# A quarter of layer 2's softmax tokens moved onto the partitions in three of sixteen samples

## The chip, the core and the metric

The kernel runs on one core of a Trainium2 chip. The metric is the device time of one launch in microseconds (us). The engines have short names here: TensorE (PE; its weight loads are PEld), VectorE (DVE), ScalarE (ACT), GpSimd (POOL), SyncE (SP). SP issues most of the DMA transfers, ACT issues some, POOL issues the gathers.

## The reference, cut to what matters

A batch of 16 samples of 64x64 tokens with 256 channels goes through four residual layers. Layer 0 replaces each token by its nearest of 1024 codes and adds it, layer 1 is attention along image rows with a sigmoid, layer 2 is the one changed here, and layer 3 is linear attention. Each layer starts with a group norm.

```python
def _L2_conv_ref(x, w1, b1, w2, b2, w3, b3):
    n = h * w                                     # 4096 tokens
    x0 = jnp.einsum('bnc,c->bn', xf, w1) + b1[0]
    x1 = jnp.einsum('bnc,c->bn', xf, w2) + b2[0]
    x2 = jnp.einsum('bnc,c->bn', xf, w3) + b3[0]
    sim = x0[:, :, None] * x1[:, None, :]
    sm = jax.nn.softmax(sim, axis=1)
    feats = jnp.einsum('bn,bnm->bm', x2, sm)
    gate = jax.nn.sigmoid(feats).reshape(b, h, w, 1)
    return gate * x
...
x = x + _L2_conv_ref(_gn(x), ...)
```

For each token m the kernel needs two sums over all 4096 tokens n: the denominator, sum of exp(x0[n]*x1[m] - max), and the numerator, the same sum weighted by x2[n]. That is 4096 x 4096 exponentials for each sample.

## The kernel before, in words

Everything is written with the Tile framework: the program is traced once as a flat list of instructions, and an offline scheduler then fixes one order for each engine's queue. On the chip each queue is worked off in that order, and an instruction waits there for what it needs. The trace order comes from generators (one for each stage of each sample) which a heap at the end of `tile_net_kernel` interleaves by due times: about one sample's time of `stage1` (layer 0, "search"), `layer1`, `rows2` and `stage2` (layer 2's rows and exponentials, "exps"), `gate2` and `stage3` (layer 3). In the middle of the run, stages of up to four samples are in work at once. At the start only the search and the exponentials overlap. At the end, sample 15 has nothing behind it.

- `stage1`, lines 398 to 415: for each of 32 token tiles, four f32 products of 512 columns into a two-bank PSUM tile `pd` (L403), a bias row on ACT (`nn`, L398), two DVE passes (L409, L414) and a gather by POOL (L415). The two-bank tiles come from the pool `ps_w`, which has two buffers; `layer1` takes its `ph` and `po` from it as well.
- `rows2`: x0, x1, x2 of a sample as three rows. `x01` holds x0 and x1 with tokens on the partitions (token tile T in column T), and the rows go to DRAM (`rd`).
- `spread_rows` (L613 to L617): loads half the tokens (2048) of x0 and of x2, each repeated over all 128 partitions, as `x0b` and `x2b`.
- `stage2` (from L620): for each half h and each token tile T, ACT computes `ex` = exp(x0 * x1[m] - max) for the 128 tokens m of the tile on the partitions and 2048 tokens n along the free axis, summing as it goes (L645, `den`); DVE multiplies by `x2b` and sums (L648, `num`). The tile `ex` has three buffers. So one sample has 64 pairs of one ACT and one DVE instruction. I call such a pair an exponential and its product. After them come `gate` (L656 to L663), a transpose (L666) and a store to DRAM (L669), from which `gate2` reads it back (L695).
- Samples 0 to 14 compute their gate once at the end (`parts=1`). Sample 15 goes in eight parts of four token tiles, each through both halves, so that its `gate2` can start early.
- `layer1` (L482, `pfg`) and `rows2` (L593, `pr`) have products with 32 output columns, which stand beside each other in four groups of PSUM partitions.

Of the kernel before, what the change touches and what calls it, by code (L numbers as in the profile page):

```python
# [9 lines left out]
F32 = mybir.dt.float32  # L10
BF16 = mybir.dt.bfloat16
U32 = mybir.dt.uint32
AF = mybir.ActivationFunctionType
ALU = mybir.AluOpType
AX = mybir.AxisListType

P = 128
C = 256
NK = C // P
TOK = 4096  # L20
NT = TOK // P
CH = 4
NCHUNK = NT // CH
CW = CH * P
# [12 lines left out]
LAG4 = 0.04  # L37
LEN3 = {0: 0.4, 1: 0.33, 2: 0.37}
FILL = ((0.05, 0.95, 2), (1.0, 1.27, 3), (1.4, 1.58, 2))
EARLY = sum(n for _, _, n in FILL)  # L40


@with_exitstack
def kernel(
# [7 lines left out]
    nc = tc.nc  # L52
# [3 lines left out]
    const = ctx.enter_context(tc.tile_pool(name="const", bufs=1))  # L56
# [5 lines left out]
    s2p = ctx.enter_context(tc.tile_pool(name="s2p", bufs=1))  # L62
# [7 lines left out]
    def bank(name):  # L70
        return ps_m.tile([P, 512], F32, tag="pm", name=name)

    def wide(name):
        return ps_w.tile([P, 1024], F32, tag="pw", name=name)
# [40 lines left out]
    PARTS = 3  # L115
# [16 lines left out]
    def busy(t, n):  # L132

        for _ in range(n):
            nc.tensor.matmul(
                t[:, :512], lhsT=ones3, rhs=ones3.unsqueeze(1).to_broadcast([P, 4, P]), start=True, stop=True,
                skip_group_check=True,
            )

    h_row, qv_row, x_row = row_tile("h_row"), row_tile("qv_row"), row_tile("x_row")  # L140

# [425 lines left out]
    def rows2(b):  # L567
        tag = f"r2_{b}"
        scale, nmean, _ = norm2[b]
        with tc.high_priority(offset=URGENT):  # L570
            pb = bank(f"pbr_{tag}")
            busy(pb, 3)
            for k in range(NK):
                nc.scalar.activation(
                    wrow_n[:, k, :].rearrange("p (j n) -> p j n", n=32)[:, :, 0:3],
                    wrow_raw[:, k : k + 1, 0:3].to_broadcast([P, 4, 3]), AF.Copy, scale=scale[:, k : k + 1],
                )
            for k in range(NK):
                nc.tensor.matmul(
                    pb[:, 0:1], lhsT=wrow_n[:, k, :], rhs=nmean[:, k : k + 1], start=(k == 0), stop=(k == NK - 1)  # L580
                )
            brow_n = small.tile([P, 1], F32, tag="brow_n", name=f"brow_{tag}")
            nc.scalar.activation(brow_n, pb[:, 0:1], AF.Identity, bias=brow)
        x01 = small.tile([P, NT, 2], F32, tag="x01", name=f"x01_{tag}", bufs=2)
        rd = dram.tile([3, 2, 4, CW], F32, tag="rows", name=f"rows_{tag}", bufs=3)
        for h in range(2):
            pr = bank(f"pr_{tag}_{h}")
            for j in range(4):
                xt = xb.tile([P, NK, CW], F32, tag="xb", name=f"xr_{tag}_{h}_{j}")
                nc.sync.dma_start(out=xt, in_=x2_d[b][4 * h + j])  # L590
                part = slice(32 * j, 32 * j + 32)
                for k in range(NK):
                    nc.tensor.matmul(  # L593
                        pr[part, :], lhsT=wrow_n[:, k, part], rhs=xt[:, k, :], start=(k == 0), stop=(k == NK - 1)
                    )
            rows = s1p.tile([P, CW], F32, tag="t4", name=f"rows_{tag}_{h}", bufs=3)
            nc.scalar.activation(rows, pr, AF.Identity, bias=brow_n)
            for n in range(3):
                nc.scalar.dma_start(out=rd[n, h], in_=rows[n : n + 97 : 32, :])
            pt = bank(f"prt_{tag}_{h}")  # L600
            for t in range(CH):
                nc.tensor.transpose(pt[:, t * P : (t + 1) * P], rows[:, t * P : (t + 1) * P], ident)
            nc.vector.tensor_copy(
                x01[:, 16 * h : 16 * h + 16, :].rearrange("p (j t) n -> p j t n", t=CH),
                pt.rearrange("p (t j n) -> p j t n", j=4, n=32)[:, :, :, 0:2],
            )
            yield 4
        rows_d[b] = x01, rd, [spread_rows(rd, b, 0)]

    def spread_rows(rd, b, h):  # L610

        x0b = s2p.tile([P, TOK // 2], F32, tag="x0b", name=f"x0b_{b}_{h}", bufs=2)
        x2b = s2p.tile([P, TOK // 2], F32, tag="x2b", name=f"x2b_{b}_{h}", bufs=2)  # L613
        for dst, n in ((x0b, 0), (x2b, 2)):
            nc.sync.dma_start(
                out=dst, in_=rd[n : n + 1, h, :, :].rearrange("o j n -> o (j n)").to_broadcast([P, TOK // 2])
            )  # L617
        return x0b, x2b

    def stage2(b, parts=1):  # L620

# [5 lines left out]
        nc.vector.tensor_reduce(ext[:, 1:2], x01[:, :, 0], AX.X, ALU.min, negate=True)  # L627
        ab = small.tile([P, 2], F32, tag="ab", name=f"ab_{tag}", bufs=1)
        nc.gpsimd.partition_all_reduce(ab, ext, P, bass_isa.ReduceOp.max)
        nmax = small.tile([P, NT], F32, tag="nmax", name=f"nmax_{tag}", bufs=1)  # L630
        nc.vector.tensor_scalar(nmax, x01[:, :, 1], ab[:, 0:1], -1.0, ALU.mult, ALU.mult)
        nc.vector.scalar_tensor_tensor(nmax, x01[:, :, 1], ab[:, 1:2], nmax, op0=ALU.mult, op1=ALU.min)
        den = small.tile([P, 2, NT], F32, tag="den", name=f"den_{tag}", bufs=1)
        num = small.tile([P, 2, NT], F32, tag="num", name=f"num_{tag}", bufs=1)
        halves.append(spread_rows(rd, b, 1))
        gd = dram.tile([NT, P], F32, tag="gate", name=f"gd_{tag}")
        gates_d[b] = gd
        yield 2
        rest = gate2(b) if parts > 1 else None
        for part in range(parts):  # L640
            those = range(part * NT // parts, (part + 1) * NT // parts)
            for h, (x0b, x2b) in enumerate(halves):
                for T in those:
                    ex = s2p.tile([P, TOK // 2], F32, tag="ex", name=f"ex_{tag}_{h}_{T}", bufs=3)
                    nc.scalar.activation(  # L645
                        ex, x0b, AF.Exp, bias=nmax[:, T : T + 1], scale=x01[:, T, 1:2], accum_out=den[:, h, T : T + 1]
                    )
                    nc.vector.tensor_tensor_reduce(  # L648
                        out=ex, in0=ex, in1=x2b, scale=1.0, scalar=0.0, op0=ALU.mult, op1=ALU.add,
                        accum_out=num[:, h, T : T + 1],  # L650
                    )
                    yield 2.4
            n = len(those)
            cols = slice(those[0], those[0] + n)
            gate = small.tile([P, NT], F32, tag="gate", name=f"gate_{tag}_{part}", bufs=1)[:, 0:n]
            nc.vector.tensor_tensor(gate, den[:, 0, cols], den[:, 1, cols], ALU.add)  # L656
            nc.vector.reciprocal(gate, gate)
            nsum = small.tile([P, NT], F32, tag="nsum", name=f"nsum_{tag}_{part}", bufs=1)[:, 0:n]
            nc.vector.tensor_tensor(nsum, num[:, 0, cols], num[:, 1, cols], ALU.add)
            nc.vector.tensor_tensor(gate, gate, nsum, ALU.mult)  # L660
            nc.scalar.activation(gate, gate, AF.Exp, scale=-1.0)
            nc.vector.tensor_scalar(gate, gate, 1.0, None, ALU.add)
# [270 lines left out]
    b = 0  # L933
# [71 lines left out]
```

## Time and profile before

| | |
|---|---|
| median of 3 runs | 5671.16 us (5653.28 to 5692.56) |
| the profiled execution | 5674.06 us, span of its instructions 5672.1 us |
| busy PE, DVE, ACT, POOL | 91%, 89%, 81%, 32% of the span |
| mean granted TensorE clock | 0.962 of full speed |
| DMA | 1059 MB, mean 187 GB/s |
| exponentials of sample 0, first to last start | 322 to 582 us |
| exponentials of sample 14 | 4958 to 5216 us |
| exponentials of sample 15 | 5224 to 5505 us |

The profiled execution takes 2.9 us more than the median. "Busy" is the share of the span in which an engine had an instruction in work. Matmuls are pipelined, so the mean duration of one is longer than what it takes from the engine; the busy time of a group divided by its count is the better price in a stream. An f32 product is recorded as two matmul instructions, a bf16 product or a transpose as one.

### The profile page before, as it was taken

To read this page: it belongs to the slowest core of one execution; us is meant where nothing else is said; L and a number is where in the kernel's file an instruction comes from. 1 tells how busy PE (TensorE), PEld (TensorE's weight loads), DVE (VectorE), ACT (ScalarE), POOL (GpSimd) and SP (SyncE) were. 2 spreads that over 40 slices of the span, in tenths; PEclk is the share of its full clock that TensorE was granted. 3 is DMA by queue.
4 is the path that set the end of the run, shared out by engine and by line. 5 is a ranking of instruction groups with operands and counts; after the bars stand their busy time and mean duration, and the time that the engine had idled before them with its cause. 6 is when DMAs were issued, how large, how long until landed. Compare 5 with 4: busy or idle time off the path is not lost.

```text
span 5672.1 us, 76096 instructions
## 1 busy us (share of the span) xinstructions
PE 5162.0 (91%) x26927; PEld 3189.6 (56%) x26927; DVE 5049.3 (89%) x7186; ACT 4571.1 (81%) x6642; POOL 1801.5 (32%) x1076
## 2 busy tenths in 40 slices
PE   7977889989999999999999999999999999987788
PEld 3534446545656566565655656565565656564556
DVE  7589799899999999999999999999999999988882
ACT  4468589888989898888978888898888879887873
POOL 2223234323333333334333333333333333321221
PEclk9988999999999999999999999999999999998889
DMA  8553744655665757566575656657575675745543
GB/s 254 174 178 84 232 115 144 214 163 185 196 198 175 224 159 236 171 211 198 185 234 155 216 185 200 210 173 236 160 224 183 201 219 156 222 149 176 200 157 119
DMA packets 521365, 1059.26 MB, mean 187 GB/s; under 512 B 52504, under 2 KB 266392, under 8 KB 512792
## 3 DMA queue, kind: packets, MB, share of 16 engines
q1 hardware_dynamic: 406288, 885.11, 46.5%
q0 software_dynamic: 73728, 67.14, 8.3%
q10 hardware_dynamic: 40968, 102.13, 4.6%
q8 instruction: 214, 3.51, 0.3%
q14 instruction: 167, 1.37, 0.1%
HBM read 751.18 MB, written 303.04 MB: 186 GB/s over the span
## 4 chain that ended last, share of the span: by engine, by line
PE 46%; DVE 17%; ACT 16%; issue 6%; DMA 5%; POOL 4%; SPq 0%; ACTq 0%; DVEq 0%; POOLq 0%
PE pd_s L403 14%; ACT ex_s L645 7%; DVE ex_s L648 7%; PE ph_l L493 4%; PE pxo_s L908 3%; PE pqv_s L782 3%; PE po_l L533 2%; PE pk_s L765 2%; ACT nn_s L398 2%; POOL qv_s L802 2%; PE pz_s L857 2%; DVE i_s L414 2%; DVE nn_s L409 2%; PE pxo_s L902 2%; PE pvr_s L865 2%
## 5 line engine op out<-in xcount | busy, mean ns | idle before, releaser
L648 DVE CUSTOM_DVE_ANT_0 ex_s<-ex_s,x2b 128x2048 f32<-128x2048 f32 x1024 | 2360.4, 2312 | 77.6 <-ACT ex_s L645 74.6
L645 ACT ACTIVATE ex_s<-x0b,nmax_s,x_r 128x2048 f32<-128x2048 f32 x1024 | 2138.6, 2089 | 40.7 <-DVE num_s L648 30.5
L403 PE MATMUL pd_s<-e,xn_s 128*128 128x512 f32 x4096 | 1971.1, 614 | 43.9 <-DVE m L409 27.9
L415 POOL DMA_INDIRECT xc_s<-in_emb_rows,i_s x512 | 1113.7, 2175 | 1852.7 <-DVE i_s L414 1337.5
L403 PEld LDWEIGHTS pd_s<-e,xn_s 128*128 128x128 f32 x4096 | 745.8, 195 | 778.8 <-issue 669.1
L409 DVE CUSTOM_DVE_ANT_0 nn_s<-pd_s,nn_s 128x1024 f32<-128x1024 f32 x512 | 619.9, 1212 | 113.5 <-PE pd_s L403 63.0
L414 DVE FIND_INDEX8 i_s<-m,nn_s 128x8 uint32<-128x1024 f32 x512 | 622.9, 1217 | 0.0
L398 ACT ACTIVATE nn_s<-ne,nx_s 128x1024 f32<-128x1024 f32 x512 | 582.5, 1143 | 33.1 <-DVE nx_s L369 18.7
L493 PE MATMUL ph_l<-wh_l,xt_l 128*128 128x256 f32 x2048 | 519.6, 390 | 28.7 <-DVE m L409 16.9
L782 PE MATMUL pqv_s<-wqv_s,xk_s 128*128 128x256 f32 x2048 | 489.3, 381 | 0.0
L493 PEld LDWEIGHTS ph_l<-wh_l,xt_l 128*128 128x128 f32 x2048 | 379.7, 192 | 138.9 <-issue 69.0
L782 PEld LDWEIGHTS pqv_s<-wqv_s,xk_s 128*128 128x128 f32 x2048 | 389.1, 191 | 120.6 <-issue 59.7
L802 POOL TENSOR_TENSOR qv_s<-qv_s,qm_s 128x512 f32<-128x512 f32 x128 | 221.6, 1731 | 662.6 <-DVE qm_s L801 363.2
L868 POOL TENSOR_TENSOR lrs_s<-lrs_s,mhalf 128x4 f32<-128x4 f32 x128 | 178.0, 1391 | 677.2 <-ACT lrs_s L867 663.3
L756 POOL TENSOR_TENSOR qv_s<-qv_s,qd_s 128x512 f32<-128x512 f32 x128 | 214.4, 1675 | 249.0 <-DVE qd_s L755 132.0
L533 PE MATMUL po_l<-blk,h_l 128*128 128x128 f32 x2048 | 282.1, 288 | 3.0 <-DVE m L409 1.5
L533 PEld LDWEIGHTS po_l<-blk,h_l 128*128 128x128 f32 x2048 | 260.6, 200 | 41.1 <-issue 24.5
L908 PE MATMUL pxo_s<-wctx_s,qo_s 128*128 128x256 f32 x1024 | 269.2, 386 | 2.2 <-DVE qo_s L876 2.2
L765 PE MATMUL pk_s<-xk_s,wk_s 128*128 128x512 f32 x512 | 256.0, 620 | 1.0 <-DMA xk_s<-x_g 0.9
L913 ACT COPY y_s<-pxo_s 128x512 f32<-128x512 f32 x256 | 147.5, 580 | 132.4 <-PE pxo_s L912 116.0
L378 PE MATMUL pt_s<-ident,xc_s 128*128 128x128 f32 x1024 | 156.7, 282 | 105.2 <-DMA xc_s<-in_emb_rows,i_s 79.0
L351 ACT ACTIVATE sq_s<-xt_s,first 128x512 f32<-128x512 f32 x256 | 200.2, 806 | 37.2 <-DMA x0b<-rows_r 21.0
(206 smaller groups left out, 7322.0 us busy)
## 6 DMA issues: line engine op xcount, KB each, us to landing
xs_s<-in_xT SPq DMA_DIRECT2D x128, 512.0 KB
xt_s<-in_xT SPq DMA_DIRECT2D x128, 512.0 KB
xc_s<-in_x SPq DMA_DIRECT2D x128, 512.0 KB
x_s<-xt_s ACTq DMA_DIRECT2D x128, 512.0 KB
xt_l<-x_s SPq DMA_DIRECT2D x128, 512.0 KB
x_l<-xt_l SPq DMA_DIRECT2D x128, 512.0 KB
xr_r<-x_l SPq DMA_DIRECT2D x128, 512.0 KB
xg_g<-x_l SPq DMA_DIRECT2D x128, 512.0 KB
```

Of the source, the lines that this page charges most:

```text
L398: nc.scalar.activation(nn, ne2, AF.Identity, bias=nx2[ch][:, t : t + 1])
L403: nc.tensor.matmul(pd[:, cols], lhsT=xn[ch][:, k, t * P : (t + 1) * P], rhs=e2[:, k, cols], start=(k == 0), stop=(k == NK - 1),)
L409: nc.vector.tensor_tensor_reduce(out=nn, in0=pd, in1=nn, scale=1.0, scalar=-3.0e38, op0=ALU.add, op1=ALU.max, accum_out=m8[:, 0:1],)
L414: nc.vector.max_index(i8, m8, nn)
L415: nc.gpsimd.indirect_dma_start(out=xc[ch][:, t, :], out_offset=None, in_=emb_rows, in_offset=bass.IndirectOffsetOnAxis(ap=i8[:, 0:1], axis=0),
L493: nc.tensor.matmul(ph[:, t, :], lhsT=X[:, k, t * P : (t + 1) * P], rhs=wh_n[:, k, :], start=(t % 2 == 0 and k == 0), stop=False, skip_grou ...
L533: nc.tensor.matmul(po[:, m : m + P], lhsT=h[:, t, k * P : (k + 1) * P], rhs=at[:, t, :, :].rearrange("p r i -> p (r i)"), start=True, stop ...
L645: nc.scalar.activation(ex, x0b, AF.Exp, bias=nmax[:, T : T + 1], scale=x01[:, T, 1:2], accum_out=den[:, h, T : T + 1])
L648: nc.vector.tensor_tensor_reduce(out=ex, in0=ex, in1=x2b, scale=1.0, scalar=0.0, op0=ALU.mult, op1=ALU.add, accum_out=num[:, h, T : T + 1],)
L765: nc.tensor.matmul(pk, lhsT=wk_n[:, k, :], rhs=xt[:, k, :], start=(k == 0), stop=(k == NK - 1))
L782: nc.tensor.matmul(pqv[:, j, :], lhsT=xt[:, k, t * P : (t + 1) * P], rhs=wqv_n[:, k, :], start=(j == 0 and k == 0), stop=False, skip_group ...
L908: nc.tensor.matmul(px[:, j, :], lhsT=qT[:, t * P : (t + 1) * P], rhs=wctx[:, 1, :], start=False, stop=False, skip_group_check=True,)
```

## The change

In samples 0, 14 and 15 the last 1024 of the 4096 tokens n (K = 8 token tiles) leave the pairs of `stage2`. The second half's `x0b` and `x2b` are loaded with 1024 columns, and its 32 exponentials and products have 1024 columns instead of 2048. The 1024 tokens are laid on the partitions instead, in eight tiles of 128:

- `parts_of_rows`: x1, x0 of those tiles and the negated maximum are put side by side (`cat`), transposed by PE, and split into three bf16 parts on DVE (`bits`). Seven transfers write them to DRAM with runs of 128 bf16 values, and four bring the x0 parts and ones into `spread`.
- `begin`: for each chunk of 512 tokens m (eight in a sample), four transfers bring the 12 rows of parts into `uu` (two buffers), once for each group of partitions.
- `outer`: the exponent x0[n]*x1[m] - max[m] as a bf16 product with 12 rows of depth, two of 512 columns into one two-bank tile `pet` of `ps_w`; four such tiles a chunk.
- `powers`: ACT takes the exponential of such a bank pair, 1024 columns from PSUM, into a tile `et` that uses the three buffers of `ex`; two such tiles a chunk.
- `contract`: eight f32 products with 32 output columns (x2 and ones), four groups of PSUM partitions beside each other, then an ACT copy.
- `collect`: four transposes and a small DVE reduction into `sums`.

Samples 1 to 13 keep the old form; `den` and `num` become slices of `sums` for all samples, and the two additions of L656 and L659 become reductions.

```diff
+SHARE = 0
+SHARES = {0: 8, 14: 8, 15: 8}
+PROD = 12
...
-        x01 = small.tile([P, NT, 2], F32, tag="x01", name=f"x01_{tag}", bufs=2)
+        x01 = small.tile([P, NT, 3], F32, tag="x01", name=f"x01_{tag}", bufs=2)
...
+        width = TOK // 2 - (P * SHARES.get(b, SHARE) if h == 1 else 0)
...
+        def parts_of_rows():
+            nc.vector.tensor_copy(cat[:, 0:NT], x01[:, :, 1])
+            nc.vector.tensor_copy(cat[:, 2 * NT : 2 * NT + K], x01[:, NT - K :, 0])
+            nc.vector.tensor_copy(pair[:, 0:K, 0], x01[:, NT - K :, 2])
+            n = 2 * NT + K
+            pp = bank(f"pcat_{tag}")
+            nc.tensor.transpose(pp[:n, :P], cat[:, :n], ident)
+            for m in range(PARTS):
+                nc.vector.tensor_copy(bits[:n, m, :], pp[:n, :P])
+                if m + 1 < PARTS:
+                    nc.vector.tensor_tensor(pp[:n, :P], pp[:n, :P], bits[:n, m, :], ALU.subtract)
...
+        def begin(c):
+            u = s2p.tile([P, CW], BF16, tag="uu", name=f"uu_{tag}_{c}", bufs=2)
+            src = ud.rearrange("i m t p -> (i m) (t p)")[:, c * CW : (c + 1) * CW]
+            for g in range(4):
+                nc.sync.dma_start(out=u[32 * g : 32 * g + PROD, :], in_=src)
...
+        def outer(c, n):
+            pw = wide(f"pet_{tag}_{c}_{n}")
+            for r in range(2):
+                g = 2 * q + r
+                rows = slice(32 * g, 32 * g + PROD)
+                nc.tensor.matmul(
+                    pw[:, r * CW : (r + 1) * CW], lhsT=spread[rows, e, :], rhs=u[rows, :], start=True, stop=True
+                )
...
+        def powers(c, n):
+            if q == 0:
+                others[c].append(s2p.tile([P, TOK // 2], F32, tag="ex", name=f"et_{tag}_{c}_{e}", bufs=3))
+            nc.scalar.activation(others[c][-1][:, 2 * q * CW : 2 * (q + 1) * CW], banks.pop((c, n)), AF.Exp)
+
+        def contract(c):
+            pn = bank(f"pn_{tag}_{c}")
+            for e in range(K // 4):
+                for g in range(4):
+                    nc.tensor.matmul(
+                        pn[32 * g : 32 * g + 32, :], lhsT=pair[:, 4 * e + g, :],
+                        rhs=others[c][1 + e][:, g * CW : (g + 1) * CW], start=(e == 0), stop=(e == K // 4 - 1),
+                    )
+            nc.scalar.copy(others[c][-1][:, 0:CW], pn)
+
+        def collect(c):
+            pt = bank(f"pnt_{tag}_{c}")
+            for t in range(CH):
+                nc.tensor.transpose(pt[:, t * P : (t + 1) * P], row[:, t * P : (t + 1) * P], ident)
+            nc.vector.tensor_reduce(
+                sums[:, :, 2, c * CH : (c + 1) * CH].rearrange("p r t -> p t r"),
+                pt.rearrange("p (t j n) -> p t n j", j=4, n=32)[:, :, 0:2, :], AX.X, ALU.add,
+            )
...
-                    yield 2.4
+                    yield 2.4 * width / (TOK // 2)
+                    c = part + step // 8
+                    n = step % 8
+                    if K == 0:
+                        pass
+                    elif n <= K // 2:
+                        if n > 0:
+                            powers(c, n - 1)
+                            yield 1.2
+                        if n < K // 2:
+                            outer(c, n)
+                    elif n == 5:
+                        contract(c)
+                        if c + 1 < NCHUNK:
+                            begin(c + 1)
+                    elif n == 7:
+                        collect(c)
+                    step += 1
```

So one chunk spreads over eight pairs of the old loop: exponents in steps 0 to 3, their exponentials in steps 1 to 4, the sums in step 5, their collection in step 7.

## The prediction

> **What bounds the kernel now.** I read the windows view first, cut at the group norms that open layer 1, 2 or 3 of a sample, since these are points every engine passes. After the window and its length it gives each engine's busy time, the granted TensorE clock, the DMA share and GB/s.
>
> ```profile
> 322.00:493.00 171.00, 107.13 (x303) 47.95 (x301) 163.77 (x215) 130.72 (x145) 53.18 (x25) 0.83 0.42 123
> 493.00:677.00 184.00, 163.01 (x902) 93.68 (x902) 156.31 (x224) 134.76 (x194) 47.22 (x25) 0.94 0.58 176
> 2000.00:2500.00 500.00, 477.81 (x2591) 301.52 (x2590) 473.49 (x668) 438.97 (x637) 172.95 (x96) 0.99 0.61 189
> 4913.00:5190.00 277.00, 233.73 (x1343) 157.04 (x1341) 243.93 (x316) 226.25 (x335) 66.51 (x41) 0.92 0.56 184
> 5190.00:5541.00 351.00, 263.26 (x1219) 186.29 (x1218) 288.82 (x420) 265.28 (x405) 83.18 (x54) 0.86 0.50 168
> ```
>
> The engines stand as PE, PEld, DVE, ACT, POOL. In the middle (2000 to 2500) PE is busy for 96% and DVE for 95%. In the stretch where sample 0's exponentials begin (S1, to sample 1's layer 1) DVE is busy for 96%, PE for 63%. In S2 (to the norm after that layer) PE leads with 89%. In the two late ones, S4 and S5, which end at the norms that open layer 3 of samples 13 and 15, all three lie between 75% and 88%, DVE ahead. So only in S1 does one engine bound alone.
>
> Next the groups, for prices: mean ns after the busy time.
>
> ```profile
> L648 DVE CUSTOM_DVE_ANT_0 ex_s<-ex_s,x2b 128x2048 f32<-128x2048 f32 x1024 | 2360.4, 2312 | 77.6 <-ACT ex_s L645 74.6 <-issue 2.5
> L645 ACT ACTIVATE ex_s<-x0b,nmax_s,x_r 128x2048 f32<-128x2048 f32 x1024 | 2138.6, 2089 | 40.7 <-DVE num_s L648 30.5 <-DVE nmax_s L632 7.4 <-ACT xt_s L381 0.4
> L409 DVE CUSTOM_DVE_ANT_0 nn_s<-pd_s,nn_s 128x1024 f32<-128x1024 f32 x512 | 619.9, 1212 | 113.5 <-PE pd_s L403 63.0 <-ACT nn_s L398 42.7 <-PE pbr_r L579 2.7
> L398 ACT ACTIVATE nn_s<-ne,nx_s 128x1024 f32<-128x1024 f32 x512 | 582.5, 1143 | 33.1 <-DVE nx_s L369 18.7 <-DVE i_s L414 11.2 <-ACT xt_s L381 0.4
> L482 PE MATMUL pfg_l<-xt_l,wfg_l 128*32 128x256 f32 x2048 | 144.6, 389 | 6.2 <-ACT qv_s L787 3.7 <-DMA xt_l<-x_s 2.4
> L502 ACT COPY h_l<-ph_l 128x1024 f32<-128x1024 f32 x128 | 129.6, 1013 | 67.2 <-PE ph_l L498 64.9
> L498 PE MATMUL ph_l<-h_row,ones 128*128 128x512 bf16 x256 | 98.1, 383 | 0.0
> L593 PE MATMUL pr_r<-xr_r,wrow_n 128*32 128x512 f32 x512 | 91.5, 613 | 8.0 <-DMA xr_r<-x_l 7.9
> L135 PE MATMUL prow_x_s<-ones 128*128 128x512 bf16 x128 | 30.2, 379 | 0.0
> ```
>
> Last the chain that ended last, its pieces added by engine:
>
> ```text
> 325 to 500:    DVE 61%, ACT 7%,  PE 2%,  the rest issue, DMA, POOL
> 500 to 675:    DVE 14%, ACT 35%, PE 23%, DMA 20%
> 4950 to 5200:  DVE 18%, ACT 33%, PE 32%
> 5200 to 5500:  DVE 40%, ACT 14%, PE 25%
> ```
>
> I use these as weights: work that an engine gains or loses moves the end by about its share of the chain, unless it becomes the bound.
>
> **What one changed sample costs.** *DVE.* A full product is 2.31 us plus its accumulator read of 0.08, together 2.39. A half one is 1.21 (L409, 1024 columns) plus 0.08. So 32 x 1.10 = 35.2 us go. Added: `bits`, five instructions from PSUM at some 0.3 (L834, 128x128 from PSUM, has 0.289 and L809 0.340), three small copies at 0.15, eight reductions at 0.2 (L603 has 0.174): 3.6. Net -31 us. *ACT.* Full exponential 2.09 + 0.19 accumulator read = 2.28, half 1.14 (L398) + 0.19 = 1.33: 32 x 0.95 = 30.4 go. A `powers` lies between 1.01 (L502, a copy from two banks) and 1.14 (L398), I take 1.08: 34.6. Eight copies of a bank at 0.58 (L913): 4.6. Net +9. *PE.* An exponent product: 0.24 in a stream (L135, 30.2/128), 0.38 alone, below that 0.12 if the two of a bank pair, which use other rows of the array, run at once; taken 0.30: 64 x 0.30 = 19.2. A product of `contract`: L482 has 144.6/1024 = 0.14 us for one f32 product of 256 columns beside its neighbours, doubled for 512 columns 0.28; L593 gives 91.5/256 = 0.36; taken 0.28, since neighbours change group as in L482: 64 x 0.28 = 17.9. 32 transposes at 0.16 (L744, 82.7/512): 5.1. With `cat` +42.5 us, bounds 31 and 53. *SP.* 43 more issues at some 0.35 us (gate reads: 0.32) make 15 us; the two loads of 1 MB shrink to half, so bytes hardly rise.
>
> **Where it falls.** The order of both programs' queues, instruction by instruction, is the same (but for a few neighbours swapped on POOL) from the end of S2 until shortly before sample 14's exponentials. I counted the instructions between the norms and priced them as above:
>
> ```text
>                           DVE                          ACT                            PE
> S1   full products 40 -> 30: -21   full 42 -> 31, +16 powers, +3 copies: -6  +15
> S2   24 -> 2 full, 32 half: -10    22 -> 1 full, 32 half, +16, +5: +15       +27
> S4   56 -> 35 full: -53            62 -> 40 full, 12 half, +23, +5: -6       +29
> S5   83 -> 40 full, 64 half: -9    74 -> 32 full, 52 half, +41, +11: +24     +56
> ```
>
> Sample 0's pairs are put later against sample 1's search, and in S4 so much moves behind sample 13's layer 3 that S5 keeps nearly its DVE work. DVE is saturated in S1, so there -21 counts for more than its chain share of 61% (-13): I take -17. PE has 64 us free there, which hide its +15. S2: -10 x 0.14 + 15 x 0.35 + 27 x 0.23 = +10. A cross-check by throughput: PE 163 + 27 = 190 us at the 96% of the middle needs 198 us, +14. S4: -53 x 0.18 - 6 x 0.33 + 29 x 0.32 = -2. S5: -9 x 0.40 + 24 x 0.14 + 56 x 0.25 = +14, and this holds the end of sample 15, where contraction, copy, transposes and reduction (some 3.7 us) now stand ahead of the last gate. After S5 layer 3 of sample 15 (5541 to 5672) is as before. Sum -17 + 10 - 2 + 14 = +5 us, on 5674 of the profiled execution 5679, on the median 5676. With PE's bounds (31 and 53 of 42.5) the three PE terms, 29 us together, become 21 or 36, so +5 becomes -3 to +12. The whole middle costs nothing: two reductions replace two additions, 0.15 to 0.18 us each.
>
> **New waits.** The chain to the first exponents (transpose, `bits`, a store, a load) is two DMA hops; the gate's own store and read took 7.2 us from issue (597.1) to the reader's start (604.3). Until then ACT has its first two exponentials and a dozen instructions of the search in its queue, 15 us, which hide it. In SP's queue every `uu` load from the third chunk on waits for PE to finish the chunk two before; behind it stand loads of sample 2's search and, in sample 14, the second store and fifth load of layer 1 of sample 15. If these come late, ACT's norms and PE's layer 1 wait next. I take 0 and bound it by 16 chunk loads x 3 us = 48 us above and nothing below. `pet` takes one of two `ps_w` buffers from the search in S1 and S2: in S1 PE waits 10 us for `m` (L409) now; taken within S2's +10, bounded by the same 10 us again.
>
> The clock rows show 0.83 in S1 and 0.86 in S5 against 0.99 in the middle. The Trainium skill, "TensorE: Matmul & The Clock Gate", Part 1 (the HAM clock gate), says that the gate only knows half and full speed and opens after some 3.4 us of sustained work; more PE work would then make the old PE work shorter. By that rule S5's 263 busy us would shrink by up to 14%, at PE's share of the chain -9 us, and the sum would be -4.
>
> Against the change speaks "DMA: Bandwidth & Descriptors", Specifications: transfers under 512 B miss line rate, and the new stores have runs of 256 B. No row here times such a store. By its fixed cost of about 2 us a transfer, an estimate from that page, the two hops are 4 us instead of 7.2, and the sum does not move.
>
> **Rivals.** *DVE bounds all four stretches.* For it: DVE is ahead in S1, S4 and S5, and 40% of the late chain is DVE. Against it: 75 to 89% for PE, and ACT loses nothing. All of -21 - 10 - 53 - 9 = -93 on the path gives 5578; two thirds of it, 5609. *The three buffers of `ex` bind (slower).* An `et` tile holds a buffer from its first `powers` to `contract`, the second to `collect`. So in two or three of each eight steps one buffer is left, and ACT and DVE must take turns: 24 chunks x 2.5 steps x 2.3 us less a quarter for half width is 104 us if nothing else stands between, 52 if every second is filled. ACT already waited 14.5 us on the product in S1 and S2:
>
> ```profile
> ACT ex_s L645 <- DVE num_s L648: 14.5, 16, 1.6
> ```
>
> Columns: total, times, longest. Against it: the queues place other work between those exponentials. It decides from half unfilled on; with +75 us 5746. *The transfers come late.* It isn't the sums that count but the 48 us of SP above: 5719.
>
> **How the numbers follow.** A measurement of this kernel can tell about 1% (57 us) from no change. Forecast (no change to tell): 0.56. DVE rival: 0.20, faster. Buffers: 0.19, slower. Late transfers: 0.05, half on each side of the 1%. So faster 0.20, same 0.58, slower 0.22. The forecast's time is 5676; its own range, with the bounds on PE, `pd` and transfers, is 5640 to 5728. Reaching to the DVE rival's 5609 and near the buffers' 5746 leaves out some 2 in 10: 5610 to 5740.
>
> **What would show it.** Right: sample 1's layer 1 opens some 17 us earlier, its end about 7 us earlier, DVE falls below 80% in S4, PE rises above 85% in S5 with a higher clock, POOL unchanged. Wrong: waits of ACT exponentials on DVE above 60 us (buffers); waits of PE on `uu` or `spread`, or of ACT norms on `xt` (transfers); S4 and S5 together shorter by over 40 us with DVE still ahead (the DVE rival). The weights would be wrong if S5 neither grows nor shrinks although PE's work there rose by a fifth.

## The result, and the profile after

The changed kernel takes 5723.77 us (median of 7 runs, 5705.56 to 5731.39) against 5671.16 us for the kernel before on the same chip (median of 7 runs). The ratio is 1.0084, with a 95% interval of 1.006 to 1.0109: some 48 us more, 34 to 62. That is inside the forecast's range and under the 1% that it called no change to tell, but the sum had +5. The profiled execution took 5730.76 us, with a span of 5729.0.

The windows of the changed kernel, cut at the same group norms as before (S1, S2, a piece of the middle, S4, S5; columns as in the prediction). S1 opens with sample 0's first exponential, here at 319.8 us, before at 322.3:

```profile
320.00:490.00 170.00, 121.67 (x394) 50.52 (x393) 143.74 (x203) 123.08 (x144) 50.42 (x25) 0.86 0.42 121
490.00:686.00 196.00, 184.26 (x1040) 97.53 (x1041) 149.16 (x251) 149.57 (x236) 42.34 (x26) 0.97 0.54 166
2000.00:2500.00 500.00, 474.00 (x2563) 296.51 (x2562) 471.53 (x671) 434.06 (x634) 174.57 (x98) 0.99 0.60 188
4938.00:5234.00 296.00, 257.93 (x1494) 166.34 (x1493) 215.60 (x313) 221.46 (x347) 58.12 (x42) 0.92 0.51 173
5234.00:5596.00 362.00, 299.08 (x1522) 196.48 (x1520) 257.94 (x455) 285.91 (x481) 58.94 (x53) 0.90 0.49 160
```

DVE lost what it was meant to lose: 20 us in S1, 7 in S2, 28 in S4, 31 in S5 by these rows, 86 in all. No stretch got shorter by more than 2 us for it; S2 grew by 12, S4 by 19, S5 by 11. In S4 and S5 every engine but PE now has over a fifth of the stretch idle.

The groups, one form to a line, give the prices (mean ns after the busy time):

```profile
L744 DVE CUSTOM_DVE_ANT_0 ex_s<-ex_s,x2b 128x1024 f32<-128x1024 f32 x96 | 120.2, 1255 | 45.5 <-ACT ex_s L740 45.2
L740 ACT ACTIVATE ex_s<-x0b,cat_s,x_r 128x1024 f32<-128x1024 f32 x96 | 118.8, 1238 | 8.6 <-DVE sums_s L744 5.2 <-PE pn_s L710 3.2
L704 ACT ACTIVATE et_s<-pet_s 128x1024 f32<-128x1024 f32 x96 | 97.0, 1018 | 10.7 <-PE pet_s L695 10.2 <-ACT fac_s L938 0.2
L710 PE MATMUL pn_s<-et_s,pair 128*32 128x512 f32 x384 | 65.9, 630 | 1.2 <-ACT et_s L704 1.2
L695 PE MATMUL pet_s<-uu_s,spread 12*128 12x512 bf16 x192 | 41.0, 410 | 22.8 <-ACT et_s L704 19.4 <-DVE xt_l L549 2.4 <-DVE m L420 1.0
L720 PE MATMUL pnt_s<-ident,et_s 128*128 128x128 f32 x96 | 16.1, 286 | 2.8 <-ACT et_s L714 2.8
L714 ACT COPY et_s<-pn_s 128x512 f32<-128x512 f32 x24 | 13.8, 577 | 11.2 <-PE pn_s L710 10.9
```

An exponent product took 41.0/192 = 0.21 us, a product of `contract` 65.9/192 = 0.34, a transpose 0.17. Together they are 123 us of new PE work. From the waits of the whole run (total, times, longest):

```profile
DVE ex_s L744 <- ACT ex_s L740: 169.5, 142, 4.7
ACT ex_s L740 <- DVE sums_s L744: 23.9, 31, 2.4
```

Before, these two were 74.6 and 30.5. So DVE's relief came back as waits of the products on the exponentials, and the exponentials do not wait more for the products. The chain that ended last shows what stands in DVE's place. I added its pieces by engine over each whole stretch, for both kernels in the same way; in the changed kernel it doesn't reach back to S1 and S2:

```text
             before                       after
S4     PE 31%, ACT 30%, DVE 17%     PE 57%, ACT 12%, DVE 11%
S5     DVE 36%, PE 27%, ACT 15%     PE 46%, ACT 31%, DVE 13%
```

### The profile page after: what moved, and what is told of

It is laid out like the page before. It is cut to its first block, busy times and chain, and to the rows that moved or that the text cites. A ratio compares the mean times of both kernels' runs of the same rounds, so it can differ in the third digit from the quotient of the medians.

```text
span 5729.0 us, 77808 instructions
## 1 busy us (share of the span) xinstructions
PE 5253.1 (92%) x27602; PEld 3209.3 (56%) x27602; DVE 4962.7 (87%) x7234; ACT 4591.5 (80%) x6762; POOL 1764.5 (31%) x1083
## 4 chain that ended last, share of the span: by engine, by line
PE 42%; ACT 14%; DVE 10%; DMA 4%; issue 4%; POOL 3%; ACTq 0%; SPq 0%; POOLq 0%; DVEq 0%
PE pd_s L414 11%; ACT ex_s L740 6%; PE ph_l L504 4%; PE pxo_s L1021 3%; DVE ex_s L744 3%; PE pqv_s L895 3%; PE po_l L544 2%; PE pk_s L878 2%; PE pz_s L970 2%; PE pxo_s L1015 2%; PE pvr_s L978 2%; POOL qv_s L915 2%; ACT nn_s L409 2%; DVE nn_s L420 1%; DVE i_s L425 1%
## 5 line engine op out<-in xcount | busy, mean ns | idle before, releaser
L744 DVE CUSTOM_DVE_ANT_0 ex_s<-ex_s,x2b 128x2048 f32<-128x2048 f32 (+1 forms) x1024 | 2261.3, 2213 | 171.9 <-ACT ex_s L740 169.5
L740 ACT ACTIVATE ex_s<-x0b,cat_s,x_r 128x2048 f32<-128x2048 f32 (+1 forms) x1024 | 2057.0, 2009 | 47.6 <-DVE sums_s L744 23.9
L915 POOL TENSOR_TENSOR qv_s<-qv_s,qm_s 128x512 f32<-128x512 f32 x128 | 205.9, 1609 | 710.2 <-DVE qm_s L914 364.5
L869 POOL TENSOR_TENSOR qv_s<-qv_s,qd_s 128x512 f32<-128x512 f32 x128 | 196.2, 1532 | 221.9 <-DVE qd_s L868 123.2
```

What stands on the lines that cost most here:

```text
L740: nc.scalar.activation(ex, x0b, AF.Exp, bias=nmax[:, T : T + 1], scale=x01[:, T, 1:2], accum_out=sums[:, 1, h, T : T + 1],)
L744: nc.vector.tensor_tensor_reduce(out=ex, in0=ex, in1=x2b, scale=1.0, scalar=0.0, op0=ALU.mult, op1=ALU.add, accum_out=sums[:, 0, h, T : T ...
```

## The experiments

All have the changed kernel as their base unless told otherwise. The letters in the expectations stand for these theories. A: the new PE work sets the loss. D: the fixed steps of a chunk (a hop from engine to engine eight times a sample) set it, however large they are. F: transfers and SP's queue. G: ACT is the engine that holds the time after the change. H: exponent tiles take the search's PSUM buffers. B: in the first run, that what the change does in all sixteen samples costs something; in the last one, that DVE's relief is worth its share. C and E stand beside their runs.

Every kernel was compared with the kernel before, run on the same chip beside it. A ratio of 0.001 is 5.7 us. The intervals are some 0.1 to 0.25% to each side, so two experiments have to differ by some 0.3% before I call them different.

```text
                                         ratio    95% interval       us against before
the changed kernel                       1.0084   1.0060 to 1.0109   +48
no sample takes the new path             1.0013   0.9998 to 1.0027    +7
sample 0 alone                           1.0029   1.0017 to 1.0041   +16
samples 14 and 15 alone                  1.0068   1.0050 to 1.0086   +39
K = 4                                    1.0075   1.0051 to 1.0100   +43
sums as bf16 products                    1.0093   1.0071 to 1.0114   +53
exponent products twice                  1.0126   1.0112 to 1.0141   +72
preparation and transfers alone          1.0006   0.9996 to 1.0017    +3
uu three chunks ahead                    1.0090   1.0076 to 1.0105   +51
half of the powers left out              1.0074   1.0054 to 1.0093   +42
copy of the sums on DVE                  1.0080   1.0061 to 1.0099   +45
exponents in one-bank tiles              1.0128   1.0108 to 1.0149   +73
DVE's relief without the new path        0.9936   0.9915 to 0.9957   -36
```

### Which samples make the loss

```diff
-SHARES = {0: 8, 14: 8, 15: 8}
+SHARES = {}                     # first run
+SHARES = {0: 8}                 # second
+SHARES = {14: 8, 15: 8}         # third
```

> SHARES is empty: no sample takes the new path; what is left of the change is x01 with three columns, the sums tile and the two reductions per gate. Theory A (PE's added work and the places where it stands in the order make the loss): the time is that of before within 10 us (5661 to 5681), and the middle between sample 1's layer 1 and sample 14's layer 1 takes 4236 us as before, so the 17 us by which the middle grew in the profile of after are gone. Rival B (the changes that touch all sixteen samples cost something, and that is where the 17 us of the middle come from): 5680 to 5695, with the middle at 4245 to 4253.

> Only sample 0 takes the new path. Theory A: S1 -1 to -3 us, S2 +12, the rest as before: +8 to +12 us on before's time, so 5679 to 5684. If the drift of the middle is started by sample 0's new path (Theory A2): +25, 5696. Rival C (the loss is made at the end alone, and sample 0's -17 of the prediction is real and only hidden by one profile): within 5 us of before.

> Samples 14 and 15 alone take the new path. Theory A: S4 +19 and S5 +10, a little in the tail: +25 to +32 us on before, 5696 to 5703. Theory A2 (the middle's drift hangs on sample 0): the same +30 here, and the two parts together give after's +48. Rival C (DVE's relief pays at the end): within 8 us of before.

Measured: +7 us (-1 to +15), +16 (10 to 23) and +39 (28 to 49). Less the first, sample 0 costs 9 and the late pair 32; with the 7 that makes 48. The parts add up within their intervals, and the loss is made where the new path runs. Theory C falls in both its places. Theory A had 8 to 12 us for sample 0 and 25 to 32 for the pair: both measured values lie above, with intervals that still reach those figures; A2's 25 for sample 0 lies outside. The steps of the walls say the same: S2 is 198 us with sample 0 alone, and S4 is 305 with the late pair alone.

The 17 us by which the middle grew in the profile of the changed kernel are another matter. Without any new path the middle took 4247 us in its profile, against 4235 before and 4253 after, which is B's number for the middle, while the time lies at A's end. In the thirteen profiles of changed kernels it lies between 4235 and 4257, with the same PE and DVE work within 0.4%. So most of those 17 us belong to no sample's new path. A part may be a real cost of the third column of `x01` and the new reductions (the +7 above, whose interval still holds zero), the rest is what one execution differs from the next. Which part is which stays open.

### Half the tokens

```diff
-SHARES = {0: 8, 14: 8, 15: 8}
+SHARES = {0: 4, 14: 4, 15: 4}
```

> K is 4 in place of 8 in all three samples: 512 tokens on the partitions, half the exponents, powers and f32 sums, but the same transfers, bits, copies and transposes. Theory A (the price is PE work of outer and contract, which halves): half of after's loss, +20 to +28 us, 5691 to 5699. Rival D (the price is in the fixed steps of a chunk: waits of the queues at the transfers, at the copy and at the transposes): at least +40, 5710 or more. Rival E (buffers of ex): with one et tile a chunk in place of two the loss falls to under +10.

Measured: +43, within the interval of the whole change. Theory E falls, since one `et` tile a chunk in place of two gives nothing back. By its text theory D was met; but the text forgot that half the tokens also bring half of DVE's relief. That had to be known first, and the last experiment measures it.

### The transfers

```diff
 # preparation alone: full width, and of the steps only the loads
+        width = TOK // 2
...
-                    elif n <= K // 2:
-                        ...
                     elif n == 5:
-                        contract(c)
                         if c + 1 < NCHUNK:
                             begin(c + 1)
-                    elif n == 7:
-                        collect(c)
```

> The new path's preparation alone: transpose of cat, bits, the eleven transfers of the parts and the 32 loads of uu per changed sample, while all exponentials and products stay full width and exponents, powers, sums and collection are left out. Theory A: +0 to +8 us on the kernel with SHARES empty, so 5681 to 5690. Rival F (SP's queue and the waits on transfers carry the loss): +25 to +40 on it, 5706 to 5722.

```diff
 # loads three chunks ahead
-name=f"uu_{tag}_{c}", bufs=2)
+name=f"uu_{tag}_{c}", bufs=4)
...
-            begin(0)
+            for c in range(3):
+                begin(c)
...
-                        if c + 1 < NCHUNK:
-                            begin(c + 1)
+                        if c + 3 < NCHUNK:
+                            begin(c + 3)
```

> uu has four buffers and its loads are issued three chunks ahead, so that a load in SP's queue waits for PE's block four chunks before and no longer two. Theory A: within 6 us of after, 5718 to 5730. Rival F: the waits of SP on the exponent products (20 us each in samples 0 and 14 in after's trace) go, and the time falls by 15 to 40 us, to 5684 to 5709.

The first cost nothing that can be told (+3 us, -2 to +10): the transposition of `cat`, `bits`, the two hops and 43 issues a sample are hidden. In that run no load waits for an exponent product, so it says nothing of such waits. The second run does, and didn't help (+51). SP's waits on the exponent products, in its own queue, first in the changed kernel, then with the earlier loads:

```profile
SPq L683 <- PE pet_s L695: 70.4, 14, 20.1
```

```profile
SPq L683 <- PE pet_s L695: 39.0, 8, 9.5
```

They fell by 31 us and no time came of it; 39 us of them are left. Theory F's ranges are out in both runs, and with them the forecast's rival of late transfers.

### More and less PE work

```diff
 # sums as bf16 products
-    pair = const.tile([P, 8, 32], F32, name="pair")
+    pair = const.tile([P, 8, 32], BF16, name="pair")
...
-s2p.tile([P, TOK // 2], F32, tag="ex", name=f"et_{tag}_{c}_{e}", bufs=3)
+s2p.tile([P, TOK // 2], BF16, tag="ex", name=f"et_{tag}_{c}_{e}", bufs=3)
...
-            nc.scalar.copy(others[c][-1][:, 0:CW], pn)
+            row = s1p.tile([P, CW], F32, tag="t4", name=f"row_{tag}_{c}", bufs=3)
+            nc.scalar.copy(row, pn)
+            others[c].append(row)
```

> The exponentials of the tokens on the partitions are kept as bf16 and their sums are bf16 products in place of f32 ones (numbers less precise; the copy of the sums goes to a tile of its own). In after's trace the 192 f32 products took 65.9 us; 192 bf16 products over as many columns (the exponents) took 41.0, so PE should lose some 25 us or more over the three samples. Theory A (PE's added work sets the loss): time falls by 12 to 25 us against after, to 5699 to 5712. Rival D (fixed steps and queue order): within 6 us of after, 5718 to 5730.

```diff
 # exponent products twice
             for r in range(2):
...
-                nc.tensor.matmul(
+                for _ in range(2):
+                    nc.tensor.matmul(
```

> Every exponent product is issued twice into the same bank: 192 more bf16 products at 0.21 us, 41 us of PE work over the three samples and nothing else. Theory A: the time grows by 20 to 40 us against after, to 5744 to 5764. Rival D: PE has 38 to 63 us idle in each of the late stretches, which hide it: under +8, 5724 to 5732.

More work cost its price: the second set of exponent products brought their group from 41.0 to 67.6 us, and the time rose by 24 us (8 to 40) over the changed kernel, in theory A's range and at the edge of D's "under +8". By the walls of the two profiles it stands in S1 (+9), S4 (+8) and S5 (+12). Less work brought nothing: the sums fell from 65.9 us to this group,

```profile
L710 PE MATMUL pn_s<-et_s,pair 128*32 128x512 bf16 x192 | 23.1, 424 | 5.1 <-ACT et_s L704 5.1
```

43 us less, and the kernel is no faster than the changed one (1.0093 to 1.0084). Its window of S5 shows where the 43 us went:

```profile
5241.00:5608.80 367.80, 298.47 (x1436) 201.01 (x1436) 256.38 (x455) 287.41 (x481) 63.01 (x53) 0.84 0.49 158
```

PE is busy for 298 us as with the f32 sums, with 86 recorded products fewer, at a granted clock of 0.84 instead of 0.90. If I take the new groups away from PE's busy time in S1, S2, S4 and S5, the old PE work there is 774 us without a new path, 740 in the changed kernel and 768 with bf16 sums. So what the cheaper sums saved in new work came back as 28 us of longer old work, at a lower clock. That f32 sums bring a higher clock is not shown by this: taken in the same way, the old work is 755 us with the exponent products twice, which has the most PE work of all, and 751 with DVE's relief alone, which has no new PE work. Why the clock was low with bf16 sums stays open. This run also put the copied sums into a tile of the search's pool (`t4`, three buffers), and what that costs was not measured apart. Theory A as I had written it (so many us less work, so many us less time) fails on this run, where D's "within 6 us" is met, and holds on the other.

### ACT's part

```diff
 # half of the powers left out: four of eight token tiles, summed twice
-                    elif n <= K // 2:
+                    elif n <= K // 4:
...
-                        if n < K // 2:
+                        if n < K // 4:
...
-                        rhs=others[c][1 + e][:, g * CW : (g + 1) * CW],
+                        rhs=others[c][1][:, g * CW : (g + 1) * CW],
```

> Exponents and their exponentials are made for four of the eight token tiles only; the sums still take eight products a chunk, the last four of them over the first four tiles again (512 tokens a sample are left out and 512 counted twice). ACT loses 48 instructions of 1.01 us (48 us over the three samples), PE 96 exponent products (20 us), DVE nothing. Theory G (after the change ACT is the engine that the exponentials go by: DVE's relief turns into waits of products on exponentials, which rose from 75 to 170 us): the time falls by 25 to 45 us against after, to 5679 to 5699. Theory A or D (PE, or the fixed steps of a chunk): by under 15 us, 5709 or more.

```diff
 # copy of the sums on DVE
-            nc.scalar.copy(others[c][-1][:, 0:CW], pn)
+            nc.vector.tensor_copy(others[c][-1][:, 0:CW], pn)
```

> The copy of a chunk's sums out of PSUM goes from ACT to DVE: 24 instructions of 0.58 us, 14 us, leave ACT's queue, and DVE, which has 38 to 104 us idle in each late stretch, takes them. Theory G (ACT paces): 5 to 15 us faster than after, 5709 to 5719. Theory D (the hops between the engines cost, whoever makes them): within 5 us of after, 5719 to 5729.

With 48 us less on ACT and 31 less on PE the time is +42, not told apart from +48; moving the copy gives +45. The windows of the first one, S2, S4 and S5:

```profile
493.80:677.70 183.90, 169.86 (x997) 94.71 (x997) 136.98 (x234) 132.43 (x214) 43.01 (x25) 0.96 0.59 177
4913.00:5214.80 301.80, 257.25 (x1509) 165.31 (x1508) 231.22 (x340) 228.81 (x364) 58.58 (x42) 0.93 0.52 171
5214.80:5583.50 368.70, 292.98 (x1441) 194.46 (x1441) 240.47 (x428) 251.29 (x428) 62.23 (x53) 0.86 0.48 156
```

In S2 the 12 us of loss are gone; there the powers mattered. But S5 has 35 us less ACT work than the changed kernel (251 for 286) and 17 less DVE work, and takes 7 us more; S4 takes 6 us more. So ACT's load alone is not what holds the end, and theory G falls for S4 and S5. As with the bf16 sums, PE's busy time in S5 hardly fell (293 us for 299), though its new groups there have 34 us in place of 52: the clock was 0.86 for 0.90. In this S5 PE waited 27 us for the eight gates of sample 15, against 14 in the changed kernel, with its queue standing behind each transpose of a gate: the queues' order moved a wait there.

### The search's PSUM buffers

```diff
-            pw = wide(f"pet_{tag}_{c}_{n}")
+            pw = [bank(f"pet_{tag}_{c}_{n}_{r}") for r in range(2)]
...
-            nc.scalar.activation(others[c][-1][:, 2 * q * CW : 2 * (q + 1) * CW], banks.pop((c, n)), AF.Exp)
+            for r, pe in enumerate(banks.pop((c, n))):
+                nc.scalar.activation(others[c][-1][:, (2 * q + r) * CW : (2 * q + r + 1) * CW], pe, AF.Exp)
```

> The exponents go to two one-bank tiles of the pool with four buffers in place of one two-bank tile of the pool with two, which the search and layer 1 use; ACT takes them in 192 instructions of 512 columns in place of 96 of 1024, at some 0.58 us, about 14 us more over the three samples. Theory H (an exponent tile that waits for ACT holds one of the search's two buffers, and that eats the gain in S1): sample 1's layer 1 opens 8 to 15 us earlier than in after, at 475 to 482 us, and the time falls by 5 to 20 us. Theory G: 5 to 15 us slower than after, 5729 to 5739, and S1 as in after.

Sample 1's layer 1 opened at 486.9 us, 3 us earlier than in the changed kernel. But in this profile the first exponential of sample 0 started at 325.7 us and not at 319.8, and what lies ahead of it is not touched by the edit: in the profiles at hand it starts anywhere from 318 to 327 us. Counted from there, S1 is 8.7 us shorter (first the changed kernel, then this one):

```profile
319.76:489.66 169.90, 121.57 (x394) 50.22 (x392) 143.77 (x202) 123.01 (x142) 50.66 (x25) 0.86 0.42 121
325.67:486.87 161.20, 123.53 (x398) 51.39 (x398) 143.62 (x203) 124.10 (x159) 51.32 (x25) 0.85 0.45 127
```

In four kernels without exponent products in sample 0, S1 counted so takes 170.6 to 172.5 us, so 8.7 is more than profiles differ by; one of the four starts late as well, at 326.5 us, and takes 172.5. Theory H's 8 to 15 us are there in S1, at their low end: the exponent tiles on the search's buffers had eaten most of what DVE's relief was worth in S1. H falls in the whole time, which went up by 25 us over the changed kernel (7 to 43). That meets G's sign, but the place does not fit it: S5 is 28 us longer (390 for 362), and ACT has 2.5 us more work in it. PE's longest wait in total is there this one, with 14.3 us in the changed kernel's S5:

```profile
PE pgt_s L780 <- DVE gate_s L777: 30.8, 8, 8.0
```

PE's waits of exponents on the powers fell in that S5 from 15.5 to 5.9 us. In the run with half of the powers both moved the same way (7.3 and 27.4 us). Why the gates came later was not taken apart.

### DVE's relief alone

```diff
 # SHARES = {}, and in samples 0, 14, 15 the second half's product is half as wide
+                    w = width // 2 if h == 1 and b in (0, 14, 15) else width
                     nc.vector.tensor_tensor_reduce(
-                        out=ex, in0=ex, in1=x2b, ...
+                        out=ex[:, :w], in0=ex[:, :w], in1=x2b[:, :w], ...
```

> The kernel with SHARES empty, but in samples 0, 14 and 15 the product of the second half takes 1024 of its 2048 columns (1024 tokens are left out of the numerator); the exponentials stay whole. DVE loses 32 x 1.1 = 35 us per sample, as by the change; ACT has 2 % less than in the changed kernel, and PE gets nothing. So this is the gain of the change without its price. Theory B (the relief of DVE is worth its share of the chain or more, and PE's part and the steps between the engines cost the rest): 35 to 70 us faster than before, 5602 to 5637. Theory G (ACT and the queues' order hold the time, DVE's relief is worth little): 0 to 20 us faster, 5652 to 5672, and the groups show the products' waits on exponentials up by 60 us or more, as in after.

This gives the gain without the price: 36 us faster than before (24 to 48), 44 us (30 to 58) faster than the same kernel with full products. It meets theory B at its lower end; G's "worth little" falls in the time, though its sign in the groups (waits of products on exponentials at 122.6 us, up 42) shows in part. First the windows of the kernel with no new path, then those of this one (S1, S2, S4, S5):

```profile
320.00:491.70 171.70, 109.42 (x303) 48.94 (x301) 163.78 (x215) 130.78 (x145) 53.68 (x25) 0.81 0.41 122
491.70:680.20 188.50, 167.05 (x903) 94.64 (x903) 156.70 (x224) 135.24 (x193) 47.20 (x25) 0.92 0.56 173
...
4927.10:5208.10 281.00, 237.14 (x1343) 159.70 (x1342) 243.54 (x316) 226.21 (x337) 63.73 (x41) 0.91 0.53 182
5208.10:5554.90 346.80, 260.38 (x1221) 184.58 (x1220) 288.89 (x420) 264.86 (x409) 82.95 (x54) 0.87 0.50 170
```

```profile
320.00:487.40 167.40, 105.55 (x300) 47.09 (x298) 153.90 (x212) 125.96 (x140) 51.35 (x25) 0.83 0.41 122
487.40:659.40 172.00, 157.91 (x903) 90.10 (x904) 133.15 (x225) 138.65 (x197) 42.41 (x25) 0.98 0.62 189
...
4907.20:5189.40 282.20, 236.07 (x1343) 159.70 (x1342) 227.55 (x325) 229.98 (x339) 61.85 (x42) 0.91 0.53 183
5189.40:5504.30 314.90, 250.98 (x1221) 180.25 (x1221) 239.86 (x410) 259.09 (x404) 71.23 (x53) 0.90 0.55 186
```

The gain lies in S5 (32 us) and S2 (16); S1 gives 4 at most and S4 nothing. Against this kernel the changed one is 1.49% longer, 84 us, with some 18 to each side: that is what the new path costs. By the walls, 24 of them are in S2, 13 in S4 and 47 in S5; the two profiled executions are 99 us apart, and the rest of that lies in S1, the middle and the tail. The whole holds better than its parts: DVE loses 16 us in this kernel's S4 and 49 in its S5, but 28 and 31 in the changed one, which also puts the work in another order and gives DVE some 11 us of small steps.

The windows show what these 84 us are. In S5 PE is busy for 299 us in the changed kernel and 251 here, and idle for 63 and 64: the 47 us are PE's longer busy time, one for one. S2 is alike, 24 us for 26 of busy time. In S4 it is 13 for 22, and in S1, with 62 us of PE idle here, 3 for 16. So the 64 us of PE's idle time in S5 were no room for new work. It fits that the run with bf16 sums, with PE as busy in S5 as before, gained nothing there. This compares profiles; why PE's idle time stays, no run shows.

Nor does the relief by itself put PE on the chain: PE has 36% of S4 here as with no new path (36%), and 38% of S5 (29% with no new path). The 57% and 46% of the changed kernel came with the new work.

With the relief known, the other runs can be read again. I add 44 us of relief (22 for K = 4, which assumes half) and take 7 off for what no new path has: the price beside the new PE groups is then 58 us beside 74 us of PE work (K = 4), 79 beside 92 (half the powers), 90 beside 83 (bf16), 85 beside 123 (the change), 109 beside 152 (twice). Each has some 18 us to either side. The price rises with the PE work: a line through the five has about half a us for one us, and some 35 us left at no PE work, both loosely held. That the hops between the engines make this remainder is only argued: the transfers don't (+3), ACT's load doesn't (S4, S5), and no run had the hops without the work. The queues' other order is a rival that no run had alone either.

## Why the prediction was right, and where its sum was wrong

The time lies in the forecast's range and under its 1%, but the sum's +5 was 43 us short of +48. The gain was right as a whole, with its parts in the wrong places; the price was sized at less than half. By stretch the forecast was -17, +10, -2 and +14 (S1, S2, S4, S5), and the profiles show -1, +12, +19 and +10. So S2 and S5 came out as forecast, but by luck: each is a gain and a price, both far larger than the terms that were added. The time lies inside the range by luck as well. With PE's bounds alone the sum was -3 to +12; the room up to +48 came from the transfers' 48 us and the buffers' rival, and neither happened.

**The work.** Right within a few us. DVE: -93 in the four stretches by the table, -86 measured. ACT: +27, measured +23. PE's 127 us were 123, with the errors against each other: exponents 0.21 for 0.30, sums 0.34 for 0.28, near the higher end of its bounds. The half exponential was 1.238 us for 1.14, the power 1.018 for 1.08, so ACT's balance of a sample stayed at 10. The price of 1.14 came from an instruction with one column as its operand; the exponential has two, bias and scale. The Trainium skill, "ScalarE: Activation LUTs", section "What ACT_TABLE_LOAD costs", gives 186 ns plus 0.833 ns a column and 93 ns for each such operand: 1.13 with one, 1.23 with two and 1.04 with none, as estimates from that page. The rows agree within some 2% (1.143, 1.238, 1.018).

**The gain: right in sum, wrong in place.** The DVE terms, -17, -1.4, -9.5 and -3.6, make -32, and relief alone measured -36 to -44. But S1, "DVE is saturated in S1, so there -21 counts for more", gave 1 to 4 us. The 61% taken as DVE's share there is near the share of the 142 us that the chain covers in that window of 175 (62%); of the whole window it is 51%. Relieved of 20 us, DVE waits for 26 us in the changed kernel's S1, of which 9.8 for the search's products and 7.4 for exponentials. Most of this was the change's own doing: with the exponents off the search's buffers the same relief made S1 some 10 us shorter than before. S5, weighted 0.40 on a small loss of DVE work, gave most of the gain: 32 us for 49 us of DVE work in the kernel with relief alone.

**The price: the term that failed.** PE and ACT terms were +11.5 in S2, +7 in S4, +17 in S5, together 36; the runs show 84 (66 to 102). The step that failed is "I use these as weights": shares of the chain before, 0.23 to 0.32 for PE, were multiplied with 112 us of PE work. The price was PE's longer busy time one for one in S2 and S5, some 0.6 in S4 and under 0.2 in S1; over all, 84 us on 123 us of new PE work is 0.68 for one. PE's shares of the changed kernel, 0.57 and 0.46, would have been nearer but still short: on the forecast's own work in S4 and S5, ACT's included, they make 49 us, where its sum has 25 and the walls show 60.

**Nothing for the rest.** "The whole middle costs nothing" and the reductions of all samples at 0.03 us each: +7 us by the medians, -1 to +15, so not refuted; the 17 us of the one profile are not the change's.

**The covers held.** S1 is no longer than before, with 15 us more PE work in it. The two hops and the transfers cost nothing in the run that had them alone, and their bound of 48 us was not needed. In the changed kernel's sample 0 the first store was issued at 333.6 us and the first exponent product started at 345.0, so the two hops took 11.4 us with their issues: more than the 7.2 of the gate's, and far more than the 4 that were estimated from the skill's page. `pet` on the search's buffers was worth 9 us in S1, inside the 10 that were allowed, but the sum had counted it within S2's +10 and nothing in S1.

**The rivals.** DVE bounding all stretches: DVE's relief is worth 36 to 44 us of its -62 to -93, and the new path eats it. Three `ex` buffers: its sign was waits of exponentials on DVE above 60 us; they fell to 23.9, and half the tiles a chunk changed nothing. The time lies between the forecast's and that rival's 5746, by another mechanism. Late transfers: out by two runs.

**The clock.** Here a rule was weighed that would have made the sum -4. The Trainium skill, "TensorE: Matmul & The Clock Gate", Part 1, says that PE's activity opens the gate. The changed kernel agrees in kind (S1 0.83 to 0.86, S2 0.94 to 0.97, S5 0.86 to 0.90), and its old work has some 34 us less busy time than in the kernel without the new path. The other runs don't follow PE's load so simply: S5 has 0.84 with bf16 sums, where PE is busy for 81% of it, 0.87 with the exponents twice (85%), and 0.90 with the relief alone (80%). No stretch of the changed kernel became shorter by more than 2 us. Whether the price of 0.68 would be higher without the higher clock, no run shows.

**The signs.** Of "what would show it", these came: DVE below 80% in S4 (73%), the higher clock. These did not: layer 1 of sample 1 opened 3.5 us earlier and not 17, its end came 8 us later and not 7 earlier, and PE in S5 rose to 83%, not over 85%. POOL was not unchanged: its busy time fell from 83 to 59 us in S5. The sign that was to show wrong weights, an S5 that neither grows nor shrinks, did not come either (+11 us), and the weights were wrong all the same.

## What to carry to other kernels

A share of the critical chain before is a poor price for an edit that takes work off one engine and gives much to another. Here the new work cost the second engine's longer busy time one for one in two of four stretches, though that engine had 64 us of idle time in one of them. Before building such an exchange, run the relief without its price (leave the work out): here the most that could be won was 36 to 44 us for 123 us of new PE work, which left little room. And when an engine at 96% is relieved and its stretch stays as long, look for what the change itself put in the way: in S1 it was the buffers that the exponents took from the search. When times from a profile's start are compared, count from an event that the change can't have moved: here the start alone differs by up to 8 us between profiles.

## What the runs showed of the hardware

The time of the unchanged kernel goes with the granted clock of its run. In the 62 runs of the kernel before beside the experiments, on four chips, the mean clock lay between 0.958 and 0.965 and the time between 5662 and 5699 us, with 3.8 us less for every 0.001 of clock (correlation -0.70). Less PE work need not make PE less busy: with 43 us of f32 products saved by cheaper ones, PE's busy time in S5 stayed at 298 us, with the clock down from 0.90 to 0.84; the cause is open. And the tail, with the same 593 products in each kernel, is busy for 113 us at a clock of 0.97 in some profiles and 121 us at 0.90 in others.
